# Kept weight splits, tile places modulo 512 bytes, later closes and conditional routed blocks in a two-layer expert kernel

## Chip, cores and metric

The kernel runs on one core of a Trainium2 chip. The metric is the device time of one execution in microseconds (us); the time of a kernel is the median of its runs. Engines are written as in the profile: PE multiplies matrices (PEld is its weight load), DVE, ACT and POOL work on vectors, SP only issues DMAs.

## What is computed

Two layers, each a "condition" network followed by a feed-forward network, on x of shape 32 x 128 x 512 (32 sequences of 128 tokens, 4,096 tokens).

```python
# layer 0, condition: one shared expert (1024 wide) and 8 routed ones (256 wide), top 2 per token
shared = (silu(x @ sw1.T) * (x @ sw3.T)) @ sw2
s = sigmoid(x @ router_w.T + t_bias);  top2 = top_k(s + router_bias, 2)
routed = sum over the two of gate * gelu(x @ rw1[e].T) @ rw2[e].T
cond = (shared + routed) / 3
# layer 0, feed-forward: one of 8 experts for each whole sequence, chosen by a small policy network
h = gelu(cond @ W1[sel] + b1[sel]);  r = h @ W2[sel] + b2[sel]
x = x + cond + 0.3 * (r @ Wo + bo)
# layer 1, condition: token shift, 16 experts of 256 slots each by a hash of the token
xk, xr = mixes of x with its predecessor
y = relu(xk[slots of e] @ w_key[e]) ** 2 @ w_value[e];  out = sigmoid(xr @ w_recept) * y
# layer 1, feed-forward: a recurrence over the 32 sequences
f, i, g = gates of (out[t], c);  c = f * c + i * g
x = x + tanh(out @ wo.T + c_final @ uo.T + bo)
```

## The kernel before

Everything is float32. Each operand of a product is split into a high part in float32r, rounded by ACT (L62), and the rest, subtracted by DVE (L63), and each product is three matmuls, high-high, high-low and low-high (`mm3`, L70). On PE a matmul of 128 x 128 by 128 x 512 is the usual unit; a DMA or a split has to bring its operands first.

The stages, in the order of time:

- **First shared half**: groups 0 to 3 of 512 tokens go through the shared expert in eight chunks of 128 hidden units each. `shared` runs over the chunks; a chunk is `up` (24 matmuls, tiles p), an activation (sg, as), and `down` (12 matmuls, acc) one chunk later. A chunk's weights (three pieces of 256 KB) are fetched from memory (`fetch_sw`) and split (`split_sw`) anew in every group, into the two-buffer pools swu and swd. Beside it run the router, the choice of the two experts (`choose`) and the slots of layer 1 (`slots`).
- **Routed experts**: the token slots are sorted by expert and padded to whole blocks of 128, at most 71 (`NBLK`). Turn i of a loop over 72 holds `r_up(i)` (pur), `turn_x(i + 1)` (transposes ptx of gathered rows), `r_down(i - 1)` (por) and `turn_h(i)` (pth). Which expert a block has is read from a register at run time; the loop always runs all 71 blocks. The split weights of all eight experts lie in r1 and r2, 64 KB a partition each. In turn 61 the loop also fetches and splits x of group 4 and the first chunk of the second half.
- **Second shared half**: groups 4 to 7, chunks 32 to 63. Between its matmuls `combine` adds shared and routed parts, and in the last group `policy` chooses the sequences' experts on DVE; the first weights of the next stage are gathered by POOL and split by `split_w` (wB).
- **Layer-0 feed-forward and closes**: a loop over sequences b, `up` and `down` for the halves a and b (pu, po), `bend` (transposes, gelu), `turn_r` (transposes into rT). For each pair of sequences `close` multiplies by Wo (pb) and mixes (dx, xk), `mix_r` makes xr, `send_k` (ptB) stores rows of xk and `send_v` (pv) multiplies xr by w_recept. wB weights are split again only where the expert changes, in a conditional on ACT and DVE.
- **Layer-1 experts** (phD, poD) and **scan** (ps_c, ps_i, ps_f with weights u on cT and w on z; poF): 16 experts by 8 weight pieces, then 32 steps.

Tiles come from pools stacked from the left or the right end of SBUF; a pool's place follows from the sizes of those before it. `shifted` makes a tile 128 bytes (`LINE`, counted in float32) longer and begins it 64 bytes in (`SHIFT`). The order of the instructions on each engine is that of the program text as a scheduler of the language arranges it; waits are semaphores it adds. [...]

Of the kernel before, what the change touches and what calls it, by code (L numbers as in the profile page):

```python
# [28 lines left out]
E0 = 8  # L29
# [8 lines left out]
NBLK = (2 * N + E0 * (P - 1)) // P  # L38
EPS = 1e-9
# [3 lines left out]
LINE = 128 // 4  # L43
SHIFT = LINE // 2
# [3 lines left out]
def tile_kernel(ctx: ExitStack, tc: tile.TileContext, a: dict, out: bass.AP):  # L48
# [7 lines left out]
    def shifted(pool, n, **kw):  # L56

        return pool.tile([P, n + LINE], FR, **kw)[:, SHIFT : SHIFT + n]
# [66 lines left out]
    blk_e = const.tile([P, NBLK], I32, name="blk_e")  # L125
    hl = const.tile([P, KD, NB], F32, name="hl")
# [10 lines left out]
    pad = const.tile([P, SHIFT], F32, name="pad")  # L137
# [7 lines left out]
    with ExitStack() as sa:  # L145
        kw = dict(reuse_waits="tile")
        raw_p = sa.enter_context(tc.tile_pool(name="raw_p", bufs=6, **kw))
        swu = sa.enter_context(tc.tile_pool(name="swu", bufs=2, **kw))
        swd = sa.enter_context(tc.tile_pool(name="swd", bufs=2, **kw))
        xh = sa.enter_context(tc.tile_pool(name="xh", bufs=KD, **kw))  # L150
        xgp = sa.enter_context(tc.tile_pool(name="xgp", bufs=3, **kw))
# [6 lines left out]

        NSW = KF * NG
        sw_raw, sw_hl, x_raw, xhl = {}, {}, {}, {}  # L160

        def fetch_sw(n, which=range(3)):
            if n < NSW:
                sw_raw.setdefault(n, {}).update(
                    {i: fetch(a["sw"][n % KF, i], f"swr_{n}_{i}") for i in which}
                )

        def split_sw(n, which=range(3)):
            if n < NSW:
# [23 lines left out]
        def shared(groups, pools, hook, done, mid=None, before_last=None, more=False):  # L193
# [36 lines left out]
            for n in range(first, last + 1):  # L230
# [11 lines left out]
                if c == KF - 2 and (g < groups[-1] or more):  # L242
# [8 lines left out]
        with ExitStack() as s0:  # L251
# [22 lines left out]
            s1, ps_x, ps_u = ExitStack(), None, None  # L274
            srt = s0.enter_context(ExitStack())
# [155 lines left out]
            def choose():  # L431
# [40 lines left out]
                nc.vector.tensor_tensor(end, first, nblk, ALU.add)  # L472
                base = rtile([P, E0], "base")
# [44 lines left out]
            def slots():  # L518
# [31 lines left out]
                nc.gpsimd.dma_start(out=res_d[NSLOT:, :], in_=zero)  # L550

# [28 lines left out]
            def hook2(g, c):  # L580
# [4 lines left out]
                if g == 1 or (g == 2 and c < 5):  # L585
# [3 lines left out]
                    if g == 2 and c == 4:  # L589
# [5 lines left out]
                        r12.append(rw_p.tile([P, 2, E0 * RCOL], FR, name="r1"))  # L595
                        r12.append(rw_p.tile([P, 2, E0 * RCOL], FR, name="r2"))
# [30 lines left out]
        with s1:  # L627
# [6 lines left out]
            def r_up(i):  # L634
                with tc.issue_after(last_up[0]) if last_up else nullcontext():
                    e = nc.tensor.value_load(
                        blk_e[0:1, i : i + 1], min_val=0, max_val=(E0 - 1) * RCOL
                    )
# [25 lines left out]

            for i in range(NBLK + 1):
                if i < NBLK:
                    r_up(i)
                    turn_x(i + 1, bx, "xb")
                    take(i + 3)
# [1000 lines left out]
```

## Time and profile before

| | us |
|---|---|
| median of three runs (2558.79 to 2566.84) | 2561.73 |
| the profiled execution | 2564.9 |
| its span, first to last instruction | 2563.2 |

The stages by the profile's windows; "busy" is the time in which the engine worked, DMA the mean busy share of the 16 DMA engines.

| stage | us from the start | PE busy | DVE busy | ACT busy | DMA |
|---|---|---|---|---|---|
| first shared half | 0 to 303.4 | 292.9 | 236.8 | 149.7 | 0.51 |
| routed experts | 303.4 to 557.8 | 251.1 | 128.0 | 103.0 | 0.49 |
| second shared half | 557.8 to 863.3 | 285.9 | 217.5 | 133.1 | 0.72 |
| layer-0 feed-forward, closes | 863.3 to 1489.7 | 607.5 | 284.2 | 317.0 | 0.35 |
| layer-1 experts | 1489.7 to 1866.9 | 374.3 | 262.4 | 235.1 | 0.69 |
| scan | 1866.9 to 2563.2 | 669.2 | 245.8 | 166.8 | 0.21 |

In a row of the timeline, the first number is the start in us, the second the length of the merged group; matmuls overlap and their ends are modelled, so the time that a group costs is read from its start to the next group's start. In a row of groups, xN counts instructions, then come busy us and the mean ns of one. In a row of waits stand the waiting and the releasing instruction, then us in total, times, and the longest.

### The profile page before, as it was taken

Reading aid. Unit: us, or ns where it says so; the run is one execution under the profiler, and the core shown is the slowest. Engines: PE = TensorE matmul, PEld = TensorE weight load, DVE = VectorE, ACT = ScalarE, POOL = GpSimd, SP = SyncE. Lnnn points to the kernel's source line nnn. Section 1 sums busy time; section 2 is a strip of 40 time slices with the busy share of each in tenths; the row PEclk is TensorE's granted clock in tenths of the full one; section 3 lists DMA queues with packets and bytes.
Section 4 is the critical chain, followed back from the end, with each engine's and each line's share of the span. In section 5 each row is a group of like instructions: output and inputs, shape, how many; then the busy total and the mean of one; then the engine's idle time right before and its main releaser. Section 6 shows DMA issues by size and latency. Waiting matters only on the chain. (4 is left out here: it accounts for less than half of the span.)

```text
span 2563.2 us, 37388 instructions
## 1 busy us (share of the span) xinstructions
PE 2480.9 (97%) x13044; PEld 2076.7 (81%) x13044; DVE 1374.6 (54%) x2413; ACT 1104.7 (43%) x2007; POOL 437.8 (17%) x459
## 2 busy tenths in 40 slices
PE   8999999999997998999999999999999999999996
PEld 5788899987876787888887889999978888888885
DVE  7797655557767544445454477667643332333336
ACT  5445533344445544455455466666532222222214
POOL 1000022222323223333222110000010000000003
PEclk9999999999998999999999999999999999999998
DMA  5445544477777324333243287776451111111027
GB/s 179 161 132 176 169 155 151 155 230 244 268 255 246 119 87 128 100 117 111 81 139 120 93 280 241 230 228 223 140 168 42 38 37 37 37 42 46 25 74 267
DMA packets 203487, 370.01 MB, mean 144 GB/s; under 512 B 38625, under 2 KB 73489, under 8 KB 200225
## 3 DMA queue, kind: packets, MB, share of 16 engines
q1 hardware_dynamic: 151872, 263.30, 30.6%
q0 software_dynamic: 36160, 74.90, 9.9%
q10 hardware_dynamic: 15264, 29.37, 3.1%
q8 instruction: 108, 1.77, 0.3%
q14 instruction: 83, 0.67, 0.1%
HBM read 392.81 MB, written 88.13 MB: 188 GB/s over the span
## 5 line engine op out<-in xcount | busy, mean ns | idle before, releaser
L70 PE MATMUL p<-xhl,swu 128*128 128x512 f32 x1536 | 380.7, 401 | 17.9 <-DVE sg L211 7.7
L70 PEld LDWEIGHTS p<-xhl,swu 128*128 128x128 f32 x1536 | 290.4, 192 | 81.6 <-issue 8.1
L63 DVE TENSOR_TENSOR wD<-rawD,wD 128x1024 fp32r<-128x1024 f32 x128 | 156.5, 1229 | 78.6 <-ACT wD L62 78.5
L70 PE MATMUL acc<-swd,as 128*128 128x512 f32 x768 | 188.2, 392 | 2.1 <-ACT as L62 1.2
L70 PEld LDWEIGHTS phD<-xe,wD 128*128 128x128 f32 x1536 | 184.5, 190 | 1.3
L70 PE MATMUL phD<-xe,wD 128*128 128x256 f32 x1536 | 185.2, 281 | 0.0
L70 PE MATMUL poD<-wD,hD 128*128 128x512 f32 x768 | 182.7, 393 | 0.0
L70 PEld LDWEIGHTS acc<-swd,as 128*128 128x128 f32 x768 | 143.6, 188 | 34.3 <-ACT as L62 2.1
L70 PEld LDWEIGHTS poD<-wD,hD 128*128 128x128 f32 x768 | 142.0, 188 | 29.6 <-DVE hD L63 0.4
L62 ACT CAST wD<-rawD 128x1024 fp32r<-128x1024 f32 x128 | 133.1, 1047 | 55.3 <-PE poD L70 30.7
L255 POOL DMA_INDIRECT xg<-in_x_rows_dram,blk_t x71 | 67.5, 951 | 466.1 <-PE ptx L265 261.6
L1352 POOL DMA_INDIRECT y<-res_d,gat_i x32 | 32.3, 1009 | 583.1 <-DVE r L1371 504.1
L70 PE MATMUL por<-r,hbr 128*128 x426 | 117.7, 410 | 3.0 <-ACT hbr L62 2.9
L70 PE MATMUL pur<-r,xb 128*128 x852 | 118.7, 288 | 0.2
L63 DVE TENSOR_TENSOR xb<-ptx,xb 128x512 fp32r<-128x512 f32 x71 | 49.1, 691 | 112.6 <-ACT xb L62 112.6
L62 ACT CAST swu<-swr 128x512 fp32r<-128x512 f32 x128 | 75.0, 620 | 79.4 <-PE p L70 52.6
L70 PEld LDWEIGHTS pur<-r,xb 128*128 128x128 f32 x852 | 105.6, 189 | 2.0 <-ACT xb L62 0.6
L70 PE MATMUL pv<-w_recept_hl,xr 128*128 128x512 f32 x384 | 100.2, 406 | 5.9 <-DVE xr L63 5.9
L708 POOL DMA_INDIRECT o<-o_d,s_i x64 | 78.8, 1232 | 150.8 <-DVE swu L63 28.8
L70 PE MATMUL ps_f<-wf_hl,z 128*128 128x512 f32 x384 | 98.0, 402 | 1.7 <-ACT wf_hl L62 0.8
L70 PE MATMUL ps_c<-wc_hl,z 128*128 128x512 f32 x384 | 96.6, 399 | 0.7 <-ACT z L62 0.7
L70 PEld LDWEIGHTS pb<-rT,Wo_hl 128*128 128x128 f32 x768 | 92.8, 188 | 4.7 <-DVE rT L1037 3.2
(1005 smaller groups left out, 4856.8 us busy)
## 6 DMA issues: line engine op xcount, KB each, us to landing
swr<-in_sw_dram SPq DMA_DIRECT2D x192, 256.0 KB
rawD<-in_w_key_dram SPq DMA_DIRECT2D x64, 512.0 KB
rawD<-in_w_value_dram SPq DMA_DIRECT2D x64, 512.0 KB
o_d<-obr SPq DMA_DIRECT2D x71, 256.0 KB
xraw<-in_x_dram SPq DMA_DIRECT2D x32, 256.0 KB
rraw<-in_rw_dram SPq DMA_DIRECT2D x32, 256.0 KB
xc<-in_x_dram SPq DMA_DIRECT2D x32, 256.0 KB
hid_d<-o ACTq DMA_DIRECT2D x32, 256.0 KB
```

The lines of the kernel that those rows point to most:

```text
L62: nc.scalar.copy(hi, src)
L63: return nc.vector.tensor_tensor(lo, src, hi.bitcast(F32), ALU.subtract).ins
L70: done = nc.tensor.matmul(ps, lhsT=left(hl, k), rhs=right(hr, k), start=start and k + n == 0, stop=stop and 3 * k + n == last,)
L255: nc.gpsimd.indirect_dma_start(out=xg[i], out_offset=None, in_=a["x_rows"], in_offset=bass.IndirectOffsetOnAxis(ap=blk_t[:, i : i + 1], ax ...
L708: nc.gpsimd.indirect_dma_start(out=o[n], out_offset=None, in_=o_d, in_offset=bass.IndirectOffsetOnAxis(ap=idx[:, b : b + 1], axis=0),)
L1352: nc.gpsimd.indirect_dma_start(out=y, out_offset=None, in_=res_d, in_offset=bass.IndirectOffsetOnAxis(ap=gat_i[:, b : b + 1], axis=0),)
```

## The change

It has five parts.

1. **Kept shared weights.** Chunks 32 to 39 (group 4) are split into tiles that stay: four of tag `w` in the pool wh (`kept_u`, two chunks each) and two in dn_p (`kept_d`, four chunks each). Groups 5 to 7 use them again, and nothing is fetched or split for them. The four tiles lie where r1 lay; the feed-forward's wB tiles later take the same four buffers, one as each is done with. `split_sw` of chunk 32 moves from turn 61 to behind the routed stage, and x of groups 5 to 7 is fetched earlier (after chunk 3 of the group before) from group 5 on.
2. **Places.** `LINE` becomes 512 bytes, `SHIFT` stays 64, and pads and pool orders are changed. The remainders modulo 512 of the tiles that PE reads, as the built programs lay them out (moving operand / stationary operand):

| product | matmuls | before | after |
|---|---|---|---|
| p, acc (shared) | 2,304 | 96/96 | 480/480 |
| pur (routed, 256 columns) | 852 | 480/160, 480/288 | 480/32 |
| por | 426 | 480/352 | 480/480 |
| pu | 768 | 480/96 | 480/480 |
| po | 768 | 480/352 | 480/480 |
| pb (256 columns) | 768 | 160/352 | 32/480 |
| pv | 384 | 352/352, 24 of them 352/96 | 480/480, 24 of them 480/32 |
| phD (256 columns) | 1,536 | 288 or 416 / 96 or 224 | 32/480 |
| poD | 768 | 224/224, 240 of them 96/224 | 480/480 |
| ps with uc, ui | 768 | 96/96 | 480/480 |
| ps with uf, wc, wi, wf | 1,536 | 480/96 | 480/480 |
| poF with wo | 384 | 96/96 | 480/480 |
| poF with uo | 48 | 96/480 | 480/480 |

3. **Later closes.** `close` and `mix_r` move from before `down(b, "b")` to the end of the iteration, and `send_k` and `send_v` of a pair come in the following odd iteration, spread between its parts.
4. **Conditional blocks.** DVE writes the number of used blocks (`used_i`); from turn 65 on, PE, ACT, DVE and SP read it and run a turn only if `used > i - 1`. POOL's gathers stay outside, and POOL zeroes the output rows of the blocks from the 65th on in `slots`.
5. **x of group 4** is fetched in turn 55 and split in turn 61.

The diff, cut to its core:

```diff
-LINE = 128 // 4
-SHIFT = LINE // 2
+LINE, SHIFT, RIGHT = 512 // 4, 64 // 4, 480 // 4
+        KEPT = KF * (NG // 2)
         def fetch_sw(n, which=range(3)):
-            if n < NSW:
+            if n < KEPT + KF:
...
         def split_sw(n, which=range(3)):
-            if n < NSW:
+            if n >= KEPT:
+                c = n % KF
+                if n < KEPT + KF:
+                    if c % 2 == 0:
+                        kept_u[c // 2] = wh.tile([P, 2, 2, 2, KD, P], FR, tag="w", name=f"kept_u{c}")
+                    if c % 4 == 0:
+                        kept_d[c // 4] = dn_p.tile([P, 4, 2, D], FR, tag="d", name=f"kept_d{c}")
+                sw_hl[n] = kept_u[c // 2][:, c % 2], kept_d[c // 4][:, c % 4]
+            if n < KEPT + KF:
...
-                if c == KF - 2 and (g < groups[-1] or more):
+                if c == (KF - 2 if n < KEPT + KF else 3) and (g < groups[-1] or more):
                     fetch_x(g + 1)
...
+                nc.vector.tensor_copy(used_i, end[:, E0 - 1 :])
...
+                for i in range(NFULL, NBLK):
+                    nc.gpsimd.dma_start(out=o_d[i * P : (i + 1) * P, :], in_=zero)
...
+            used = None
             for i in range(NBLK + 1):
-                if i < NBLK:
-                    r_up(i)
-                    turn_x(i + 1, bx, "xb")
-                    take(i + 3)
-                if i > 0:
-                    stored = r_down(i - 1)
-                if i < NBLK:
-                    turn_h(i)
-                if i == NBLK - 10:
+                if i == NFULL + 1:
+                    e = (nc.tensor, nc.scalar, nc.vector, nc.sync)
+                    used = nc.values_load(
+                        used_i[0:1, 0:1], engines=[x.engine for x in e], min_val=NFULL, max_val=NBLK
+                    )
+                take(i + 3)
+                e = first_col(i) if i > NFULL and i < NBLK else None
+                with tc.If(used > i - 1) if used is not None else nullcontext():
+                    if i < NBLK:
+                        r_up(i, e)
+                        turn_x(i + 1, bx, "xb")
+                    if i > 0:
+                        stored = r_down(i - 1)
+                    if i < NBLK:
+                        turn_h(i)
+                if i == NBLK - 16:
                     with tc.issue_after(stored):
                         fetch_x(NG // 2)
+                if i == NBLK - 10:
                     split_x(NG // 2)
-                    fetch_sw(NSW // 2)
-                    split_sw(NSW // 2)
-                    fetch_sw(NSW // 2 + 1)
+                    fetch_sw(KEPT)
+                    fetch_sw(KEPT + 1)
...
-        wh = sw_.enter_context(tc.tile_pool(name="wh", bufs=1, side="right", **kw))
+        wh = sw_.enter_context(tc.tile_pool(name="wh", bufs=4, side="right", **kw))
...
+                if b == 0:
+                    ws[kind] = wh.tile([P, 2, KD, D], FR, tag="w", name=f"wB_{kind}")
...
+            dn_p = s2.enter_context(tc.tile_pool(name="dn_p", bufs=2, side="right", **kw))
+            split_sw(KEPT)
...
                 bend(b + 1, "a")
+            pair = b - 3 if b % 2 and 0 <= b - 3 < NB - 2 else None
+            if pair is not None:
+                send_k(pair)
+            if b + 1 < NB:
                 up(b + 1, "b")
                 used()
...
+            if pair is not None:
+                send_k(pair + 1)
             if b == NB:
                 send_v(NB - 6)
+            if 0 <= b < NB:
+                down(b, "b")
+                used()
+            if pair is not None and pair < NB - 6:
+                send_v(pair)
+            if b + 1 < NB:
+                bend(b + 1, "b")
+            if pair is not None and pair < NB - 6:
+                send_v(pair + 1)
             if j == PB - 1 and 0 <= c < NB // PB:
                 wo_done, k_done = close(c, b == NB)
...
-            if 0 <= b < NB:
-                down(b, "b")
-                used()
-            if b + 1 < NB:
-                bend(b + 1, "b")
-            if 0 <= b - 2 < NB - 2:
-                send_k(b - 2)
-                if b - 2 < NB - 6:
-                    send_v(b - 2)
```

## The prediction

> **What bounds the kernel now.** I read the page's busy shares first, then its 40 slices (PEclk is 9 in all but the last: no slow clock to win back), then the stage windows, then the waits of PE, and last the timeline of PE inside single stages.
>
> ```profile
> PE 2480.9 (97%) x13044; PEld 2076.7 (81%) x13044; DVE 1374.6 (54%) x2413; ACT 1104.7 (43%) x2007; POOL 437.8 (17%) x459
> 557.80:863.30 305.50, 285.90 (x1284) 232.07 (x1283) 217.46 (x417) 133.08 (x227) 95.73 (x100) 0.97 0.72 240
> 863.30:1489.70 626.40, 607.47 (x3227) 505.79 (x3226) 284.19 (x541) 316.99 (x701) 175.09 (x178) 0.99 0.35 113
> ```
>
> TensorE is the bound in every stage. So there are three ways to gain: fewer matmuls, a shorter distance between matmuls, and the PE idle that is left, most of it in the second shared half (19.6 us of 305.5) and in layer-0 FFN plus closes (18.9 us of 626.4). The change reaches for all three.
>
> Span 2563.2 us, its own execution 2564.9 (1.7 us around the span); the median of the three runs is 2561.7. I sum against the span and carry the difference to the median.
>
> **1. Conditional routed blocks.** The routed stage runs 71 turns of one shape; a steady one:
>
> ```profile
> 519.20 1.64 PE L70 MATMUL por<-r,hbr 128*128 x6
> 520.68 0.38 PE L652 MATMUL pth<-ident,ge 128*128 128x128 f32 x2
> 520.82 1.66 PE L70 MATMUL pur<-r,xb 128*128 x12
> 522.32 0.60 PE L265 MATMUL ptx<-ident,xg 128*128 128x128 f32 x4
> 522.68 1.65 PE L70 MATMUL por<-r,hbr 128*128 x6
> ```
>
> By starts: pur 1.50, ptx 0.36, por 1.48, pth 0.14 us. How many blocks are used follows from the inputs: the reference's top-2 of the drawn inputs gives 2559, 708, 128, 0, 373, 317, 2547 and 1560 slots, so 20+6+1+0+3+3+20+13 = 66 blocks of 128. (Of the tokens for which the expert with exactly 128 is second or third, the nearest has a margin of 0.0015 in score, so rounding does not make a 67th.) The condition `used > i - 1` runs turns 65 and 66 and skips 67 to 71: 4 pur, 3 ptx, 5 por, 4 pth = 6.0 + 1.1 + 7.4 + 0.6 = **-15.1 us**. POOL's gathers stay outside and 7 zero stores (0.95 us each if they cost what a gather does) come at some 85 us, in a stage where POOL works 12.6 us of 303.
>
> The branches: in this trace ACT and DVE take 132 each at the FFN's weights, 45 and 56 ns each with the next instruction about 0.1 us later, but they jump over a handful of instructions. PE's five jumps each pass 24 matmuls with their weight loads and register work. [...] By the row: 7 x 0.1 = 0.7 us. [...] I take **+2** (ends 0.7 and 10)[...].
>
> **2. Places modulo 512 bytes.** This is the largest term, and no operation is removed for it. One step of the scan:
>
> ```profile
> 2090.75 2.96 PE L70 MATMUL ps_c<-wc_hl,z 128*128 128x512 f32 x12
> 2093.55 2.97 PE L70 MATMUL ps_i<-wi_hl,z 128*128 128x512 f32 x12
> 2096.36 0.60 PE L1383 MATMUL ptC<-ident,c 128*128 128x128 f32 x4
> ...
> 2102.78 2.88 PE L70 MATMUL ps_c<-uc_hl,cT 128*128 128x512 f32 x12
> 2105.50 2.88 PE L70 MATMUL ps_i<-ui_hl,cT 128*128 128x512 f32 x12
> 2108.22 2.95 PE L70 MATMUL ps_f<-uf_hl,cT 128*128 128x512 f32 x12
> 2111.01 1.33 PE L70 MATMUL ps_c<-wc_hl,z 128*128 128x512 f32 x5
> ```
>
> All groups have twelve matmuls of one shape, yet by starts wc takes 2.80, wi 2.81, uc 2.72, ui 2.72 and uf 2.79 us. What differs is where the two operands lie: uc and ui at remainder 96 modulo 512 beside cT at 96; uf at 480 beside cT at 96; wc and wi at 480 beside z at 96. Over the whole trace, start to start inside a group and single stalls left out: moving and stationary operand at the same remainder 227 to 229 ns (six groups of names; pv, 352/352, 230), at a distance of 128 or 384 bytes 232 to 234, often alternating 229 and 237. The changed program puts all 512-wide pairs at 480/480. Pairs with a distance today: pu and po of the FFN, 1,536 matmuls; ps with wc, wi, wf and uf, 1,536; por 396 of those still executed; poD 240 of 768; poF with uo 48. That is 3,756 matmuls x 5.9 ns (the mean excess over 227 of these groups) = **-22 us**. The 256-wide pairs (pur, phD, pb) go to a distance of 64: in phD 64 costs 117.8 ns as 192 and 320 mostly do, but two experts at 192 run at 113.6 (192 matmuls x 4.2), and pur at 192 runs 1.3 ns faster than at 320 (some 390): **+1.3**.
>
> [...] What no row shows is 480 beside 480; 96, 224 and 352 beside themselves are near enough.
>
> **3. Second shared half (558 to 863).** From the second group on, chunks are no longer loaded and split: 24 chunks x 3 = 72 splits less on DVE (0.68 us: 49 us) and ACT (0.62: 45 us), and 18.9 MB less on SP's queue, in a stage whose DMA engines are 72% busy. PE does not shrink by that; only its waits do:
>
> ```profile
> PE p L70 <- DVE sg L211: 7.7, 1, 7.7
> PE pv L70 <- DVE xr L63: 5.9, 2, 3.0
> PE ptB L1105 <- DVE xk L1059: 4.7, 3, 2.1
> PE p L70 <- DVE xhl L63: 3.4, 2, 2.1
> PE pth L728 <- ACT o L730: 3.1, 1, 3.1
> PE pb L70 <- DVE rT L1037: 3.0, 1, 3.0
> PE por L70 <- ACT hbr L62: 2.9, 1, 2.9
> ```
>
> Here belong sg 7.7, xhl 3.4, o 3.1, and two of 1.8 and 0.6 in the last group: 16.6. The 7.7 is a chain: ACT sits 8.2 us in front of the split of wB_W1a for its gathered megabyte, the copy of `o` queues behind it, DVE's adds behind that, and `sg` behind those. The gather still comes behind the policy, which sheds about five 0.68 us splits on DVE ahead of it, and its transfer loses its rivals. I leave half of the 7.7 and the first xhl wait (the load of group 5 keeps its place): 16.6 - 3.9 - 1.3, **-11.5** (ends -4 and -17).
>
> The start is new: the kept tiles lie where r1 and r2 lay, so the split of chunk 32, hidden today behind turn 61, comes after the last turn: one ACT copy (0.62) and part of a DVE subtraction (0.69) with nothing to cover them: **+1.3**.
>
> **4. x of group 4 fetched six turns before its split.** Today both stand in turn 61: the turns from 524.29 to 537.25 take 12.96 us for two of 3.47, 6.0 lost, the 2.9 of the table among it. Four ACT copies (2.5 us) still stand between `hbr` and its predecessor, against the 1.0 us that ACT idles there in a steady turn: 1.5 stays, **-4.5**.
>
> **5. Later closes.** Today `close` runs between up and down of the same iteration whose `turn_r` made rT, and `send_k` and `send_v` follow 3 us on. The table has the price: xr 5.9, xk 4.7, rT 3.0 = 13.6. After it, down and bend (3.2 us) stand between, and the sends come three matmul groups later (8 us), more than the longest of these waits (3.1). ACT's row copies and SP's stores come in bunches of two on two buffers, 2.8 us apart, which may hold ACT once or twice: **-11** (ends -4 and -13.6).
>
> **Sum**: -15.1 + 2 - 22 + 1.3 - 11.5 + 1.3 - 4.5 - 11 = -59.5. Span 2503.7, median 2561.7 - 59.5 = **2502 us**.
>
> **Rivals.**
> *Places help in part* (480/480 behaves like 352/352, or other traffic makes the alternation): half of the 22, 2513; none, 2524. For: 230 of pv. Against: 227 at two other remainders. Chance 0.14.
> *Waits only move*: PE arrives earlier at the policy's gather and at weights of a changed expert, so 3, 4 and 5 give 8 of 27: 2502 + 19 = 2521. For: the 7.7 ends at a DMA. Against: that DMA's queue empties. Chance 0.14.
> *Slower*: [...] Without its 2 us the sum is -61.5, so it decides from 8.8 us a conditional; at 12 us the time is 2502 - 2 + 84 = 2584. [...] Chance 0.03.
> *Blocks not skipped*: needs 71 used where 66 are counted; left out.
> The forecast itself holds 0.67; mixtures of the first two, near 2530, 0.02.
>
> **Numbers.** Low ends: places at wc's whole difference, 0.08 us a group or 6.7 ns a matmul, -25; then -15.1 + 0.7 - 25 + 1.3 - 17 + 1.3 - 6 - 13.6 = -73, 2488, and 3 us for the spread of a median whose runs lie between 2558.8 and 2566.8. High ends but the slower rival: -15.1 + 10 - 10 + 1.3 - 4 + 1.3 - 3 - 4 = -24, 2538; all of them together are unlikely. The range reaches from 2485 to 2532. A measurement of this kernel tells 0.3%, 7.7 us, from no change: faster 0.95, same 0.02, slower 0.03.
>
> **What would show it.** Pur 67 turns (804 matmuls), por 66 (396); uf and wc groups at 2.72 us by starts and poD, pu, po at 227 ns; swr 120 loads; the 7.7 us wait under 4; no xr, xk or rT wait over 1 us; a gap under 5 us between the last pth and the first p. It is wrong if groups at 480/480 stay at 2.80, if PE shows several us after a jump, or if the freed waits come back under other names.

## The result and the profile after

The changed kernel takes 2536.24 us (median of four runs, 2530.64 to 2539.89); the kernel before, run beside it, 2560.93. The ratio is 0.9901, with a 95% interval of 0.9887 to 0.9914. Two later sets of runs of the same kernel gave 0.9879 (0.9864 to 0.9893) and 0.9889 (0.9872 to 0.9906). It is faster, as forecast, but by 25 us and not by 59, and it lies above the range of 2485 to 2532.

The profiled execution has a span of 2533.5 us, 29.7 less than before. These are lines of the page of the changed kernel and of its stage windows (columns: stretch, its length, then busy us of PE, PEld, DVE, ACT and POOL with their instructions, granted clock, DMA share, GB/s):

```profile
PE 2450.0 (97%) x12946; PEld 2065.7 (82%) x12946; DVE 1325.6 (52%) x2330; ACT 1059.2 (42%) x1924; POOL 432.3 (17%) x467
```
```profile
550.70:844.60 293.90, 283.01 (x1274) 231.20 (x1275) 179.93 (x344) 98.63 (x159) 83.44 (x101) 0.98 0.57 184
844.60:1467.10 622.50, 601.77 (x3227) 507.30 (x3226) 281.72 (x543) 313.60 (x701) 180.22 (x181) 0.98 0.36 115
```

DVE's and ACT's work and the loads of the second shared half have gone as they should (217 to 180 us, 133 to 99 us, DMA share 0.72 to 0.57). But PE still has 10.9 us without work in that half and 20.7 in the feed-forward stage, where it had 18.9 before. So idle time was moved, not removed. Set beside the forecast by stage:

| stage | forecast, us | measured, us | before to after |
|---|---|---|---|
| first shared half | 0 | +2.6 | 303.4 to 306.0 |
| routed experts, to the first p of chunk 32 | -15.1 + 2 - 4.5 - 2.3 + 0.5 = -19.4 | -9.7 | 254.4 to 244.7 |
| second shared half | -11.5 + 1.3 = -10.2 | -11.6 | 305.5 to 293.9 |
| layer-0 feed-forward, closes | -11 - 9.1 = -20.1 | -3.9 | 626.4 to 622.5 |
| layer-1 experts | -1.4 + 0.8 = -0.6 | -0.2 | 377.2 to 377.0 |
| scan | -9.3 | -6.9 | 696.3 to 689.4 |

(-2.3, -9.1, -1.4 and -9.3 are the forecast's 5.9 ns times the matmuls of por, of pu and po, of poD and of the scan.) Sixteen of the missing 30 us are in the feed-forward stage, ten in the routed one. The waits of PE in the changed kernel (us in total, times, longest):

```profile
PE pt_0b L1044 <- ACT ue_0b L1037: 7.2, 1, 7.2
PE p L72 <- ACT xhl L64: 6.2, 1, 6.2
PE acc L72 <- DVE as L65: 5.7, 5, 2.5
PE p L72 <- ACT kept_u L64: 4.6, 1, 4.6
PE p L72 <- DVE sg L223: 3.5, 1, 3.5
...
PE pt_6a L1044 <- ACT o L760: 2.6, 1, 2.6
PE ptB L1146 <- ACT hf_26a L1047: 2.4, 1, 2.4
PE pt_15a L1044 <- DVEq L895: 2.0, 1, 2.0
...
PE ptB L1146 <- ACT hf_16a L1047: 2.0, 1, 2.0
```

The waits for xr, xk and rT are gone. In their place stand waits for ACT in the same stage (o, and hf twice, are new; ue_0b takes 7.2 us instead of 2.8) and three kinds at the start of the second half (kept_u, sg, as).

### The profile page after: what moved, and what is told of

It reads as the page before. It is cut to its first block, busy times and chain, and to the rows that moved or that the text cites. A ratio compares the mean times of both kernels' runs of the same rounds, so it can differ in the third digit from the quotient of the medians.

```text
span 2533.5 us, 36800 instructions
## 1 busy us (share of the span) xinstructions
PE 2450.0 (97%) x12946; PEld 2065.7 (82%) x12946; DVE 1325.6 (52%) x2330; ACT 1059.2 (42%) x1924; POOL 432.3 (17%) x467
## 5 line engine op out<-in xcount | busy, mean ns | idle before, releaser
L72 PE MATMUL p<-xhl,swu 128*128 128x512 f32 x768 | 190.4, 400 | 6.2 <-ACT xhl L64 6.2
L72 PE MATMUL p<-xhl,kept_u 128*128 128x512 f32 x768 | 187.3, 399 | 8.1 <-ACT kept_u L64 4.6
L72 PEld LDWEIGHTS p<-xhl,swu 128*128 128x128 f32 x768 | 145.8, 192 | 37.4 <-ACT xhl L64 6.2
L72 PEld LDWEIGHTS p<-xhl,kept_u 128*128 128x128 f32 x768 | 144.1, 191 | 38.6 <-ACT kept_u L64 4.8
L72 PE MATMUL pur<-r,xb 128*128 x804 | 111.6, 287 | 3.2 <-DVE xb L65 1.3
L72 PE MATMUL por<-r,hbr 128*128 x396 | 108.3, 407 | 0.1
L72 PE MATMUL acc<-kept_d,as 128*128 128x512 f32 x384 | 95.2, 396 | 7.3 <-DVE as L65 5.3
L72 PE MATMUL poF<-z,wo_hl 128*128 128x512 f32 x384 | 96.5, 399 | 0.0
L738 POOL DMA_INDIRECT o<-o_d,s_i x64 | 66.7, 1042 | 172.1 <-PE pth L758 80.1
L72 PE MATMUL acc<-swd,as 128*128 128x512 f32 x384 | 95.5, 393 | 0.4 <-DVE as L65 0.4
```

The source lines that it names most:

```text
L72: done = nc.tensor.matmul(ps, lhsT=left(hl, k), rhs=right(hr, k), start=start and k + n == 0, stop=stop and 3 * k + n == last,)
L738: nc.gpsimd.indirect_dma_start(out=o[n], out_offset=None, in_=o_d, in_offset=bass.IndirectOffsetOnAxis(ap=idx[:, b : b + 1], axis=0),)
```

## Experiments

**Comparison.** Between the sets of runs the kernel before differs by 0.1 to 0.3% (2560.9 us at first, 2564 to 2568 us here), so kernels are compared by ratios, and the changed kernel was run again in two of the sets. Single profiles of it differ by up to 2 us in a stage.

> The changed kernel itself, beside the others of this call, so that they can be compared on one chip: a ratio to the kernel before of 0.990 as at first (0.9887 to 0.9914). Theory A (the stages differ from run to run by about 1 us): first shared half 306, routed 245, second shared half 294, layer-0 feed-forward 622, layer-1 experts 377, scan 689, each within 2 us. Theory B (the stages of the earlier single profile were not typical): some stage differs by 4 us or more.

> The changed kernel itself again, the reference of this call: ratio between 0.988 and 0.990, routed stage 245 to 247, second shared half 294 to 296, layer-0 feed-forward 621 to 623. Any stage 3 us or more away from these two profiles would say that the stage comparisons of single profiles can't be trusted to that size.

Measured: 2535.5 and 2535.06 us; stages 307.9 / 246.4 / 295.9 / 621.3 / 376.5 / 688.4 and 305.9 / 244.5 / 296.0 / 621.5 / 376.3 / 688.6, so theory A of the first: no stage is more than 2.1 us away. The first shared half lies between 304.6 and 310.6 in all profiles of changed kernels (303.4 in the one profile before). Where its 2.6 us come from was not tried and stays open.

### Places

```diff
-    pad = const.tile([P, 416 // 4], F32, name="pad")
+    pad = const.tile([P, 288 // 4], F32, name="pad")
```

> The changed kernel with the pad of 416 bytes made 288: all tiles of the left end move down by 128 bytes, so that p, acc of the kept half, pu, po, por and the four ps with uf, wc, wi, wf (4,620 matmuls of 512 columns) stand at a distance of 128 modulo 512, and no instruction is added. Theory A (distance costs what the two traces differ by: pua 4.6, pub 1.3, po 2.2 and 4.7, uf 6.2, wc 7.0, wi 6.9, wf 2.8, por 1.3 ns a matmul, and about 4 for p and acc): 13.7 + 0.5 + 4.6 = about 19, 2555. Theory B (the prediction's 5.9 ns everywhere): 27, 2563. Theory C (places play no part): 2536.

Measured: 0.9938 (0.9923 to 0.9954), against 0.9890 for the mean of the three ratios of the changed kernel: 12 us. Places do count, but for less than theories A and B said. These 12 us are not the part's own worth, since the pad also moves p and acc of the kept half, which stood at equal places before the change too. By stage: scan 697.2 against 688.4 to 689.4; second shared half, where p and acc are, 298.0 against 293.9 to 296.0; feed-forward 621.5 against 621.3 to 622.5, so nothing in that stage as a whole. The scan shows both behaviours. First the changed kernel, then pad_288 (PE's timeline: start, length, group):

```profile
2083.04 2.88 PE L72 MATMUL ps_f<-uf_hl,cT 128*128 128x512 f32 x12
2085.76 2.88 PE L72 MATMUL ps_c<-wc_hl,z 128*128 128x512 f32 x12
2088.48 2.89 PE L72 MATMUL ps_i<-wi_hl,z 128*128 128x512 f32 x12
2091.20 0.60 PE L1431 MATMUL ptC<-ident,c 128*128 128x128 f32 x4
2091.56 3.01 PE L72 MATMUL ps_f<-wf_hl,z 128*128 128x512 f32 x12
2094.41 0.60 PE L1424 MATMUL ptF<-ident,r 128*128 128x128 f32 x4
```
```profile
2111.26 2.95 PE L72 MATMUL ps_f<-uf_hl,cT 128*128 128x512 f32 x12
2114.05 2.96 PE L72 MATMUL ps_c<-wc_hl,z 128*128 128x512 f32 x12
2116.85 2.97 PE L72 MATMUL ps_i<-wi_hl,z 128*128 128x512 f32 x12
2119.66 0.60 PE L1431 MATMUL ptC<-ident,c 128*128 128x128 f32 x4
2120.01 3.04 PE L72 MATMUL ps_f<-wf_hl,z 128*128 128x512 f32 x12
2122.89 0.60 PE L1424 MATMUL ptF<-ident,r 128*128 128x128 f32 x4
```

From start to start uf, wc and wi take 2.72 us at equal places and 2.79 to 2.81 at a distance of 128 bytes. But wf, which comes after the transposes ptC, takes 2.85 at equal places and 2.88 at the distance. Over the trace of the changed kernel, the median times from start to start inside the wf group go 316, 233, 236, 224, 231, 236, 228, 232, 231, 227, 227 ns: the first matmul after transposes takes 89 ns more, and the next eight waver between 224 and 236. In uf, wc and wi, which stand behind other matmuls of the same kind, it is 227 throughout. Each of the groups pub, po of half a, por, wf and poF with wo follows transposes, and without their first they stay at 230 to 232 ns. The mean of before's groups at a distance (232.9 ns) had that history in it; the forecast took all of it for distance.

In the feed-forward stage even a real gain does not all arrive: an odd iteration takes 18.13 us in most cases in pad_288 and 17.95 in the changed kernel, an even one 19.1 to 19.4 in both. In the even ones ptB waits for ACT (hf): in the changed kernel 0.2 to 0.5 us in seven of them, 2.0 and 2.4 us in two.

### Later closes and Wo

old_closes puts `close`, `mix_r`, `send_k` and `send_v` back where they were (the loop's tail of the diff, reversed).

> The changed kernel with close, mix_r, send_k and send_v back in the order of the kernel before; all else as changed (2536.2 us). Theory A (in layer-0 feed-forward the later closes took the xr, xk and rT waits away, but ACT's queue and Wo's load put others in their place, so that the part is worth about 3 us): 2539, the stage of 622.5 us becomes about 625, the 7 us wait of PE for ue_0b stays, the waits for xr, xk and rT are back with 8 to 14 us and the waits for hf and o are gone. Theory B (the prediction: the part is worth 11 us and something else ate it): 2547, stage about 634. Theory C (the later closes cost time): under 2534.

> old_closes again, beside changed_third. Theory A (the trace of old_closes against the changed kernel: odd iterations 18.12 instead of 17.95 us, even ones 19.06 instead of 19.25, so nothing in the steady state, and about 5 us in the iterations with combines and changed weights): 4 to 6 us above changed_third. Theory B (the 7.7 us of the one profile): 7 to 8. Theory C (the first comparison of medians, 0.9896 against 0.9901): 0.

Measured: 2540.49 us, 0.9896 (0.9877 to 0.9914) at first, which is no difference to 0.9890; then 2544.22 us, 0.992 (0.9904 to 0.9936), beside changed_third's 2535.06, so 9 us, with intervals that just meet. The stage is 629.0 and 626.7 us against 621.3 to 622.5. The two medians do not agree; by the stage the part is worth 4 to 8 us. PE's waits in old_closes_2:

```profile
PE pt_0b L1044 <- ACT ue_0b L1037: 7.4, 1, 7.4
PE pv L72 <- DVE xr L65: 5.9, 2, 3.0
PE ptB L1146 <- DVE xk L1096: 4.1, 2, 2.1
PE pb L72 <- DVE rT L1074: 3.0, 1, 3.0
```

So 13.0 us of waits went with the later closes as forecast, and new waits for o and hf (7.0 us) came, with 0.8 us more at DVE's branches. In the steady part nothing is won: odd iterations go from 18.12 to 17.95 us, even ones from 19.06 to about 19.25. The gain lies mostly in iterations 7, 8, 26 and 28; in iteration 16 some 3.5 us of it are lost again (19.04 to 22.54 us, old_closes_2 against changed_third). And the largest wait of the stage does not depend on the closes at all. ACT's timeline of the changed kernel shows it:

```profile
847.58 0.59 ACT L1037 COPY ue_0a<-pu_0a 128x512 f32<-128x512 f32 x1 [2.07 <-issue]
855.47 1.04 ACT L64 CAST Wo_hl<-raw_Wo 128x1024 fp32r<-128x1024 f32 x1 [7.30 <-DMA raw_Wo<-in_Wo_dram]
856.53 1.28 ACT L1047 ACT_TABLE_LOAD   x1
857.83 1.37 ACT L1047 ACTIVATE hf_0a<-pt_0a,b 128x128 f32<-128x128 f32 x4
859.08 0.59 ACT L1037 COPY ue_0b<-pu_0b 128x512 f32<-128x512 f32 x1
```

ACT stands 7.3 us in front of the cast of Wo, and ue_0b, for which PE waits, stands behind it. Wo's two loads are issued at 846.0 and land 9.5 us later: from 850 to 855.5 the windows show a DMA share of 1.02 (weights of wB, hid, x, the stores of sh and the gathers of the first late block). Before, the same wait was 2.8 us. Iteration 1 went from 16.98 to 21.99 us with it.

> The changed kernel with Wo loaded and split one iteration later (and w_recept too). In the trace ACT stands 7.3 us in front of the cast of Wo, whose DMA lands 9.5 us after its issue with all DMA queues full, and hf_0a and ue_0b stand behind it. Theory A (the load in ACT's order is the cause): PE's wait of 7.2 us for ue_0b goes to under 2.5, the stage of 622.5 becomes 617 to 618, time 5 us under the changed kernel. Theory B (the DMAs as a whole are the limit, and the next wait for a load takes its place): 0 to 1 us.

late_wo only moved the two lines by one iteration (`if b == 1` and `if b == 2`). The scheduler put the cast back ahead of hf_0a, the wait was still 6.3 us, and the ratio 0.9874 (0.986 to 0.9888) says nothing about this cause. late_wo_2 binds it (`up` now returns ACT's copy of ue):

```diff
-                up(b + 1, "a")
+                ue_done = up(b + 1, "a")
...
-                wo0 = weight_b("Wo")
+                with tc.issue_after(ue_done):
+                    wo0 = weight_b("Wo")
```

> The changed kernel with Wo's load where it is, but ACT's cast of Wo held behind its copy of ue_1a (in late_wo ACT's order had stayed: the cast of Wo still stood ahead of hf_0a). Theory A (ACT's order is the cause of PE's wait of 6.5 to 7.2 us): pt_0b waits under 2.5 us, layer-0 feed-forward 616 to 618 instead of 621 to 622.5, time 4 to 5 us under the changed kernel. Theory B (loads as a whole are the limit): the wait comes back at W1b or at the next hid, under 1 us won.

Measured: 2534.53 us, 0.9873 (0.9858 to 0.9889); stage 616.8 us, 4.5 to 5.7 less. The wait for ue_0b is gone; one of 4.8 us for hb_0a (DVE) is there. So theory A holds for the stage; in iteration 1 itself the new order wins 3 us (21.7 to 22.0 us become 18.77). The whole time cannot show it: its interval meets that of the changed kernel, and in that profile the first half and the routed stage were 3 to 5 us longer.

### Conditional blocks

```diff
-                if i == NFULL + 1:
+                if False:
...
-                with tc.If(used > i - 1) if used is not None else nullcontext():
+                with tc.If(used > i - 1) if False else nullcontext():
```

> The changed kernel without its conditionals: all 71 routed turns run, unconditionally. Theory A (the seven conditionals cost about 6 us, read as 1.4 at the first, 1.1 inside turn 66 and some 3.5 for the five skipped ones, against 15.1 for the turns that they skip): 2536.2 + 15.1 - 6 = 2545. Theory B (the conditionals cost 2 us as predicted and the rest of the gap in front of chunk 32 is the late split of kept_u, which stays here): 2549. Theory C (skipping wins nothing): 2536.

Measured: 2542.29 us, 0.9909 (0.9893 to 0.9924), some 5 us above the changed kernel by the ratios, though the intervals meet. The routed stage is 254.1 us, 8 to 10 longer (theory A), but the second shared half is 290.7, 3 to 5 shorter. Skipping 15.1 us of matmuls wins 8 to 10 in its stage, so the seven conditionals cost 5 to 7 us there, and 3 to 5 us of the gain are lost behind it.

```diff
                 nc.vector.tensor_copy(used_i, end[:, E0 - 1 :])
+                nc.vector.memset(used_i, NBLK)
```

> The changed kernel with the number of used blocks set to 71, so that all seven conditionals are there and none skips; the five more blocks are rows of zeros weight. Theory A (a conditional costs what the trace shows at turns 65 and 66, 1.4 and 1.1 us): routed stage 254 + 7 x 1.2 = 262, and behind it the start of the second half gains some of it back as in all_turns: 5 to 8 us above all_turns, 10 to 14 above changed_third. Theory B (only the first, with the load of the register, costs; later ones are hidden): 2 us above all_turns, 6 to 8 above changed_third.

Measured: 2558.54 us, 0.9968 (0.9957 to 0.9979). The routed stage is 261.6 us: seven conditionals that skip nothing cost 7.5 us, 1.07 each, as theory A says. The whole time is some 20 us above changed_third's by the ratios, more than its 10 to 14. (The second half was 300.3, some 10 us longer than in all_turns: 4 of them lie at its start, 6 in group 7, where the cause was not looked for.) Conditional turns of forced_71:

```profile
542.65 0.38 PE L672 MATMUL pth<-ident,ge 128*128 128x128 f32 x2
542.78 0.48 PE L72 MATMUL pur<-r,xb 128*128 x2
544.19 1.61 PE L72 MATMUL pur<-r,xb 128*128 x10 [0.93 <-DVE xb L65]
545.64 0.60 PE L278 MATMUL ptx<-ident,xg 128*128 128x128 f32 x4
545.99 1.64 PE L72 MATMUL por<-r,hbr 128*128 x6
```

PE's first pur follows pth without a pause, over the branch. The loss is a wait for xb, two matmuls later. Four of the six turns are like this, 3.7 of the 7.5 us together. In the other two, pur itself starts 1.2 and 1.1 us late; the profile puts that down to ACT's hbr, which pur does not read, so its cause is open. DVE's timeline of forced_71 shows where the wait for xb comes from:

```profile
547.67 0.69 DVE L682 COPY obr<-por 128x512 f32<-128x512 f32 x1 [3.20 <-PE por L72]
548.28 0.68 DVE L65 TENSOR_TENSOR xb<-ptx,xb 128x512 fp32r<-128x512 f32 x1
```

Inside a conditional the copy obr stands ahead of the subtraction of xb and waits for por; in all_turns xb stands ahead. forced_71_xb_first turns this round (`turn_x` now returns DVE's subtraction):

```diff
-                        turn_x(i + 1, bx, "xb")
+                        x_done = turn_x(i + 1, bx, "xb")
...
-                        stored = r_down(i - 1)
+                        with tc.issue_after(x_done) if used is not None and i < NBLK - 1 else nullcontext():
+                            stored = r_down(i - 1)
```

> forced_71 with DVE's subtraction of xb held ahead of its copy obr in the conditional turns, as the order is in unconditional ones. Theory A (a conditional's price is mostly the order of the instructions inside it, which cannot be mixed with those of other turns): the waits of pur for xb of 0.9 us, four in all, go, the routed stage 261.6 becomes 256 to 258, and a turn 3.5 to 4.0 us instead of 4.8. Theory B ([...]): 261 to 262, a turn stays at 4.8.

Measured: 2553.02 us, 0.9945 (0.9926 to 0.9963), routed stage 261.2. The four waits for xb are gone, and two turns take 3.52 and 3.44 us from ptx to ptx instead of 4.8. But the stage did not get shorter: the next two take 7.37 and 4.42 us, and a pause of another kind came:

```profile
551.51 0.38 PE L672 MATMUL pth<-ident,ge 128*128 128x128 f32 x2
553.74 2.42 PE L72 MATMUL pur<-r,xb 128*128 x12 [1.85 <-issue]
555.95 1.05 PE L278 MATMUL ptx<-ident,xg 128*128 128x128 f32 x4
```

PE waits 1.85 us for nothing that the profile shows, and after it works at a clock of 0.66 until 558.7. So theory A is right about the waits for xb and wrong about the stage, which is as theory B has it; how the 7.5 us divide between the order and the branches stays open. (By the ratios the whole time is 6 us under forced_71's; in the profiles that is the second half, 295.4 against 300.3.)

Skipped turns are another matter. one_if puts turns 67 to 71 under a single conditional.

```diff
+                if i == NFULL + 3:
+                    nest.enter_context(tc.If(used > i - 1))
...
-                with tc.If(used > i - 1) if used is not None else nullcontext():
+                with tc.If(used > i - 1) if NFULL < i < NFULL + 3 else nullcontext():
```

> The changed kernel with one conditional over turns 67 to 71 together instead of five; turns 65 and 66 keep theirs. Theory A (each skipped turn costs PE and ACT a jump of its own, 3.5 us for five): the gap from the last pth to the first p, 5.0 us, becomes about 2.2, routed stage 243, but the start of the second half waits for its loads anyway, so that 1 to 3 us are won. Theory B (the gap is the late split of kept_u alone): gap and time unchanged.

Measured: 2536.3 us, 0.9881 (0.9865 to 0.9898). The routed stage shrinks to 242.9 us and the gap in front of chunk 32 from 5.0 to 2.0: five skipped conditionals cost 3 us more than one. The time does not change beyond its interval. The rows of one_if show why:

```profile
548.54 0.32 SPq L682 DMA_DIRECT2D o_d<-obr  x1
...
549.62 8.82 PE L72 MATMUL p<-xhl,kept_u 128*128 128x512 f32 x36 [1.62 <-ACT kept_u L64]
...
553.49 0.60 ACT L222 ACTIVATE sg<-p 128x512 f32<-128x512 f32 x1
...
554.94 1.01 POOL L741 DMA_INDIRECT o<-o_d,s_i  x1 [3.44 <-ACT sg L222]
...
560.17 0.75 DVE L757 SCALAR_TENSOR_TENSOR o<-o,g,shc 128x512 f32<-128x512 f32 x1 [6.79 <-DMA o<-o_d,s_i]
...
564.56 0.75 DVE L757 SCALAR_TENSOR_TENSOR o<-o,g,shc 128x512 f32<-128x512 f32 x1 [1.01 <-DMA o<-o_d,s_i]
565.23 0.68 DVE L223 TENSOR_TENSOR sg<-sg,p 128x512 f32<-128x512 f32 x1
...
565.96 5.25 PE L72 MATMUL p<-xhl,kept_u 128*128 128x512 f32 x12 [7.53 <-DVE sg L223]
```

ACT has chunk 32's sigmoid ready at 554.1, but DVE multiplies it (sg, which frees the p that PE waits for) only at 565.2. Ahead of it in DVE's order stand the adds of the first combine, which wait for gathered rows of `o`. The first of these gathers starts at 554.9 us (553.2 in the changed kernel), in both kernels some 6.5 us after SP issued the store of the last block. PE started chunk 32 1.1 us earlier, and what arrives earlier waits longer. The loads of chunk 34 are late too (ACT sits 8.1 us in front of them until 562.2), but DVE's adds end later. Chunk 39 starts at 623.2 us, at 623.7 in changed_again.

### Kept weights and their start

In the changed kernel the six raw buffers hold chunks 32 and 33 until the late split, so the load of chunk 34 goes out at 552.8 us, behind the loads of the first combines. From chunk 32 to 39 it takes 69.3 us (59.6 before); from there to chunk 56 it takes 147.0 (153.0 before). But the first long wait, in chunk 33, does not end at that load. The changed kernel has the same order on DVE as one_if:

```profile
555.37 0.60 ACT L222 ACTIVATE sg<-p 128x512 f32<-128x512 f32 x1 [0.79 <-issue]
...
560.76 0.75 DVE L754 SCALAR_TENSOR_TENSOR o<-o,g,shc 128x512 f32<-128x512 f32 x1 [6.35 <-issue]
...
563.49 0.68 DVE L223 TENSOR_TENSOR sg<-sg,p 128x512 f32<-128x512 f32 x1
564.23 4.60 PE L72 MATMUL p<-xhl,kept_u 128*128 128x512 f32 x12 [3.46 <-DVE sg L223]
```

In the kernel before and in all_turns, which have no conditional turns, chunk 32's first sg stands ahead of these adds on DVE (at 564.3 us and 569.4 before, 565.3 and 573.0 in all_turns). In forced_71, which has the conditionals and skips nothing, it stands behind them: there chunk 34 starts 24.2 us after chunk 32, in all_turns 18.6. So this order goes with the conditional blocks and not with arriving early. No run changes it alone.

light_start moves the combines of chunks 33 to 36 to 41, 43, 45 and 47; light_start_2 to 43, 46, 50 and 53, and it holds the first blocks' gathers and loads behind those of chunks 34 and 35. The diff is that of light_start_2, without the lines that keep the last load for `hold`:

```diff
-    n += (g == last - 1 and c == KF - 1) - (g == h and c == 0)
+    n += (g == last - 1 and c == KF - 1) - (g == h and c < 5) + ((g - h, c) in ((1, 3), (1, 6), (2, 2), (2, 5)))
...
-            get_o(flat[0], cp, 3)
-            get_o(flat[1], cp, 3)
...
+                if g == h and c in (1, 2):
+                    with tc.issue_after(last_dma[0]), tc.issue_after(hold):
+                        get_o(flat[c - 1], cp, 3)
```

> The changed kernel with the four combines of chunks 33 to 36 moved to chunks 41, 43, 45 and 47, where nothing is loaded or split any more; all work is the same. Theory A (the second half starts slowly because the loads of chunks 34 to 37 compete with the combines' loads and stores, and their splits with the combines on ACT and DVE): the 69.3 us from chunk 32 to chunk 39 become about 63, time 5 to 6 us under the changed kernel, as chunks 40 to 55 run at 8.65 us each with room to spare. Theory B (the late start of the loads, which waited for raw buffers behind the late split, is the whole cause): under 2 us won, and chunk 34 still starts 21 us after chunk 32.

Measured: 2537.85 us, 0.9891 (0.9876 to 0.9906), nothing. The start took 62.8 us as theory A says (though chunk 34 still came 21 us after chunk 32, as theory B says: the adds of `o` still stood ahead of sg), and 9 us were lost later, from chunk 39 to 56: two chunks of group 6 took 12 us, where DVE waited 5 us for a gather of `o`.

> As light_start, but the four combines go to chunks 43, 46, 50 and 53 and the gathers, shc and xc of the first two blocks are held until the shared weights of chunks 34 and 35 are fetched. Theory A (the loads of chunk 34 are late because they go out late and share the DMA engines with those 3 MB; the combines then compete on ACT and DVE): chunk 34 starts 17 us after chunk 32 instead of 20 to 21, chunk 39 60 to 62 us after it instead of 69, and with the doubles spread chunks 40 to 56 lose under 3 us, so that 5 to 8 us are won. Theory B (the load waits for raw buffers freed by the split of chunk 32, nothing else): chunk 34 still at 20 us or more.

Measured: 2533.16 us, 0.9871 (0.9856 to 0.9886). PE's longest waits from 548 to 625 us in it:

```profile
PE p L72 <- ACT kept_u L64: 4.7, 1, 4.7
PE p L72 <- DVE sg L225: 0.7, 2, 0.5
PE acc L72 <- DVE as L65: 0.5, 1, 0.5
```

Chunk 34 starts 16.0 us after chunk 32, chunk 39 59.5 us after it: the start is as fast as before the change. The half takes 290.3 us, 4 to 6 less, though group 7 gave some of it back (two chunks of 11.6 us). The ratio's interval meets those of the changed kernel. So the first combines, with their gathers and loads, make the 10 us (theory A), not the late split, which is still there. The run took the gathers and loads out of the way of both the loads of chunk 34 and DVE's sg, and does not part the two; the rows above show that DVE's adds ended later.

What keeping wins was tried three times. no_keep and no_keep_late_x fetch and split anew in groups 5 to 7, into the kept tiles:

```diff
-            if n < KEPT + KF:
+            if n < NSW:
                 sw_raw.setdefault(n, {}).update(
...
-                if c == (KF - 2 if n < KEPT + KF else 3) and (g < groups[-1] or more):
+                if c == KF - 2 and (g < groups[-1] or more):
```

(The second pair is in no_keep_late_x alone.)

> The changed kernel with its kept tiles, but fetched and split anew in groups 5 to 7 as before (72 splits each on DVE and ACT and 18.9 MB of loads are back); the tiles' places and the late start of the second half stay. Theory A (keeping is worth about 17 us from chunk 39 on, since the trace shows 6 us won in groups 5 and 6 and 11 of the 15 us in group 7 beside it, and the start costs 10): 2553, with the wait for sg of about 7 us back and the loss at chunks 32 to 38 unchanged. Theory B (the prediction's 11.5 us): 2548. Theory C (those waits were already gone for another reason): 2536.

> As no_keep, but x of groups 5 to 7 is fetched after chunk 6 of the group before, as in the kernel before, and not after chunk 3. In no_keep x held four of the six raw buffers for four chunks, and ACT waited 115 us for swr. Theory A (the 36 us over the changed kernel came mostly from those buffers; keeping itself is worth about 17 us): a ratio of 0.997, 17 us above the changed kernel, second shared half about 311. Theory B (the loads themselves are too slow beside the kept tiles): still over 1.002. Theory C (the prediction's 11.5 us): 0.9945.

Measured: 1.0041 (1.0027 to 1.0055) and 1.0039 (1.0026 to 1.0051), some 38 us above the changed kernel, and ACT's line in no_keep reads:

```profile
ACT kept_u L64 <- DMA swr<-in_sw_dram: 114.6, 52, 10.4
```

The x buffers were not the reason, as no_keep_late_x shows. ACT waits for a load in most chunks; whether the late first load or the rewriting of the kept tiles in turn keeps the loads late was not tried. Either way these two runs are no measure of the part. never_kept gives swu, swd, the early split and wB's own tiles back:

```diff
                     fetch_sw(KEPT)
+                    split_sw(KEPT)
                     fetch_sw(KEPT + 1)
...
-        ws = {}
+        ws = {k: wh.tile([P, 2, KD, D], FR, tag="w" + k, name=f"wB_{k}") for k in ("W1a", "W1b", "W2a", "W2b")}
```

> The changed kernel without keeping and with the start as before: swu and swd stay through both halves, chunk 32 is split in turn 61, groups 5 to 7 are fetched and split anew, wB has its own tiles; all products keep their remainders of 480 except xb of pur (480 too instead of 32). Theory A (late start costs 10 us, from chunk 39 on keeping wins 21, so the part is worth 11 in the second half, and 1 or 2 of the late split's gap at the end of the routed stage come back): 9 to 11 us above changed_third, second shared half 304 to 306, chunk 39 59 to 61 us after chunk 32. Theory B (what no_keep says: keeping is worth 36 us): 30 us or more above. Theory C (keeping wins nothing net): equal to changed_third.

Measured: 2552.85 us, 0.9952 (0.9936 to 0.9967), 16 to 18 us above the changed kernel. None of the three theories fits: the second half is 317.6, 22 longer, with sg waits of 7.2 and 6.1 us, and chunk 39 comes 64.6 us after chunk 32. The routed stage is 249.2, 3 to 5 longer. The feed-forward stage is 616.4, 5 shorter; there ACT stands 3.5 us in front of Wo instead of 7.3 (iteration 1 takes 17.83 us). So beside the other four parts keeping wins 22 us in the second half and costs 5 in the next stage.

The same run shows that the slow start is not of the kept tiles alone. With the early split back and the conditionals left, it takes 64.6 us; with the conditionals gone and the late split left (all_turns), 66.6; with both, 69.3; with neither (the kernel before), 59.6.

### Together

> one_if, late_wo_2 and light_start_2 together. Theory A (three places on the path, one after the other, so their gains add): 10 to 15 us under the changed kernel, a ratio of 0.982 to 0.985. Theory B (a gain at the end of the routed stage is lost in the wait for loads behind it): 8 us, 0.985 to 0.986.

> all_three with xb ahead of obr in turns 65 and 66. Theory A (1 to 2 us earlier at the end of the routed stage, which the loads of chunk 34 then take back): within 1 us of all_three, a ratio of 0.985 to 0.987. Theory B (they are kept): 2 us under all_three, 0.984 to 0.986.

all_three takes 2529.99 us, 0.9858 (0.9843 to 0.9873); all_four, with xb first in turns 65 and 66, 2526.78 us, 0.9841 (0.982 to 0.9862). Both are faster than the kernel before, and all_four is clear of the changed kernel too; all_three's interval reaches just into those of the changed kernel's two later sets. Between themselves the intervals overlap, so neither theory of all_four is decided. (In all_four's profile, of its slowest run, the second half is 295.0 us.) In all_three the routed stage is 242.7, the second half 290.1 and the feed-forward stage 618.8. That is some 2, 5 and 3 us under the changed kernel. By the ratio all_three wins 8 us, which is theory B of its expectation; a wait of 5.6 us for hb_0a is left in it.

## Why the prediction was wrong

- **Blocks.** Right in what is skipped: pur 804 and por 396, as counted. "The branches: +2" failed; 0.7 of it came from the row of ACT's and DVE's branches, the rest was the author's estimate. The conditionals cost 5 to 7 us in the routed stage and 3 to 5 us behind it (all_turns), so that the upper end of 10 would have been near. The runs show a cost that the forecast put at nothing, the order of DVE's instructions in and behind the blocks: a wait of PE for xb of 0.93 us in a turn and, by the rows, the adds of `o` ahead of chunk 32's sg. What a branch itself costs stays open; five skipped ones took 3 us more than one. The idle 5 us cost again: PE's clock, 1.00 in chunk 32 before, is 0.68 from 550.7 to 556.0. Chunk 32 takes 7.2 us there and 5.9 in one_if, where the gap is 2 us and the clock stays 1.00. The length of one gap does not tell it alone: after the 1.85 us in forced_71_xb_first the clock was 0.66 for 5 us.
- **Places.** The effect was right (uf, wc and wi at 2.72 us); the size was not: -22 against some 8 to 12. The scan won 7, layer 1 and por about 1, and the feed-forward between nothing (pad_288) and 4 (steady iterations of before against old_closes: odd 18.28 to 18.12 us, even 19.15 to 19.06). The term that failed is "3,756 matmuls x 5.9 ns". It took before's whole excess over 227 as curable, when half of these groups stand behind transposes, and those that still do are held at 230 to 232, and it charged all of it to PE's path where even iterations wait for ACT anyway (hf, 0.2 to 2.4 us in nine of them). That places count is shown by pad_288, which took 12 us more with one pad changed; why equal remainders are faster, no run shows. The +1.3 for the 256-column pairs was not seen either: in the middle of a group, pur went from 117 or 118 ns to 114.
- **Kept weights.** The net term is about right (-11.6 in the half, -10.2 forecast), but by luck: two errors cancel. From chunk 39 on 6 and 15 us were won, more than forecast, and "The start is new: +1.3" was 10. The forecast saw the split that would stand uncovered and not what was queued behind it: the first combines, whose gathers DVE waits for (6.8 us in one_if) and whose loads stand ahead of those of chunk 34. Part of the 10 belongs to the conditionals, as all_turns and never_kept show. "No slow clock to win back" missed a slice: PEclk is 8 around the 7.7 us wait too. In group 7 the granted clock was 0.91 before and is 0.98 now, and PE is busy 74.4 us there instead of 77.7.
- **x of group 4.** The two turns at its split take 9.2 to 11.4 us in the changed kernel's profiles and in all_turns, instead of 13.0: -2 to -4, and -4.5 was forecast.
- **Closes.** "-11" was 4 to 8 by the stage. All three waits went, but the forecast let nothing late come in their place; ACT's hf and o did.
- **Not foreseen.** The longer wait of ACT at Wo's cast, in front of hf_0a: +5 us in one iteration.

The rival "waits only move" described what happened, 2521 by its sum; the forecast gave its mixture with half the places (near 2530) a chance of 0.02, as though the two were unlikely together. They were not alternatives. The forecast's own sign of being wrong, freed waits that come back under other names, is what the profile after shows.

## What to carry to other kernels

When a change makes one engine arrive earlier, look for the loads and gathers that must then be earlier too: here one_if's 3 us were lost because the rows of `o` came no earlier (first gather at 554.9 us against 553.2). An engine that stands in front of a late load (ACT 7.3 us at Wo, DVE 6.8 us at the gathers of `o`) held up what stood behind it in its order, so ask of each moved or conditional piece what then stands behind what. A per-instruction gain seen in means should be taken from groups with the same history and only in stretches where that engine is the one waited for.

## What the runs showed of the hardware

- After transposes, the time from the start of the first 128x512 float32r matmul to the next start is 313 to 316 ns in the median instead of 227: in wf 313 before, at 480/96, and 316 in the changed kernel, at 480/480; in por 316 in both. At equal places eight more waver between 224 and 236 ns (wf in the changed kernel).
- At a distance of 128 or 384 bytes modulo 512 the starts alternate 229 and 237 to 238 ns (uf, wc and wi in the kernel before; in pad_288, at 128, twelve of them take 2.79 to 2.81 us); at equal remainders they are 227 (uc and ui at 96 before, at 352 in pad_288 and at 480 in the changed kernel).
- The 5 us gap in front of chunk 32 is followed by some 5 us at a granted clock of 0.5 to 0.7 (0.68 in the changed kernel, 0.51 in changed_third, 0.50 in late_wo_2); the 2 us gap of one_if is not (1.00). But in forced_71_xb_first the clock was 0.66 for 5 us after a stretch of 3.7 us in which PE worked 1.4, with a pause of 1.85 us at its end.
- In forced_71 PE goes over a conditional that does not skip without a pause in four of six turns: pur starts 0.13 to 0.14 us after pth, as in the unconditional turns of all_turns.
